# Layer 1's bias, residual and normalisation move from VectorE and GpSimd to ScalarE and GpSimd; every second unit of layer 3 has one side tap less; the final pass loads its first z tiles earlier

## The chip, the cores and the metric

The kernel runs on one core of a Trainium2 chip. Its five engines are named here as in the profile: PE (matrix products), DVE (VectorE), ACT (ScalarE), POOL (GpSimd) and SP, which only issues DMAs. Each engine executes its own instructions in order, and waits for the others by semaphores. The metric is the time of one execution on the device in microseconds (us), lower is better. A shared set of 16 DMA engines moves data between HBM and the on-chip memory (SBUF); results of PE land in PSUM.

## What is computed

The input is 16 images of 192 channels of 64 x 64 points, in float32. Four residual blocks follow one another, each with its own normalisation of the input ("norm" below: mean and inverse deviation per image and group of 6 channels):

- layer 0: x1 = x + (a small network per channel of the normalised x that ends in a likelihood);
- layer 1: x2 = x1 + W * shifts(norm(x1)) + b, where `shifts` stacks the image and its four shifts by one point, so W is five 192 x 192 products, added up;
- layer 2 (SS2D): x3 = x2 + selective scans of u = norm(x2) in four directions. Delta, B and C are projections of u; for each direction k, channel and state n = 0..15 there is a scan over the 4096 points, h = exp(delta * A) * h + (delta * u) * B, y += h * C, and u itself is added to y;
- layer 3: a depthwise convolution of norm(x3), the sum of a 3 x 3, a 5 x 5, a 1 x 7 and a 7 x 1 (29 taps together), a 192 x 192 product to z, statistics of z per channel over all 16 images, then out = x3 + min(relu(z * scale + shift), 6).

## The kernel before

**Tiling.** Two images make a pair; a pair's 2 x 192 channels lie on three tiles of 128 partitions (`NT` = 3, index j). There are eight pairs (`npair`), and L = 4096 points.

**One pair.** `pair(i)` runs `scans(i)`, the scans of layer 2, and then `layer3(i)`. The scans are 48 blocks of 1024 points x 16 states = 768 steps. One step is: the product pbt = du * pbt on DVE (pbt, B spread over the partitions, comes from PE two steps ahead, in two PSUM buffers), the scan on DVE, a copy of the last state on ACT, h * cb on POOL (cb, the C values, is loaded by SP two steps ahead), a sum over the states on PE (`ysum`), and the decay exp(delta * A) for a step three ahead on ACT. In every fourth step POOL also issues an accumulating DMA h <- h. Every 16 steps a new block begins, with a new delta and du.

**The side stream.** During the scans of pair i the front of pair i+1 runs: a Python generator that yields the work of layer 0, layer 1 (`layer1`, lines 666 to 756), the projections of layer 2, and behind these comes `ahead` of pair i (layer 3's depthwise convolution of its first tile, whose scans are done by then: matmuls with a diagonal, and a few taps `a_p` on DVE). Each step of the scans spends a credit of 1; a yield costs 1 unless it names another price: 0.52 for a matmul of layer 1, 0.57 for one of `ahead`. Work that is still left after the last step is executed behind the scans, beside nothing. Pair 0 has its front before everything else (`deep`).

**Order.** All instructions that go through an `_Engines` object with `True` are kept in program order on their engine (line 68, which is therefore the line that the profile shows for nearly all of them). The deep front, constants and the final pass are ordered by the scheduler.

**Layer 1.** The rows of x1 come in eight chunks c of 512 points (a chunk's input has ten rows, one above and one below, 640 points, 576 at the edges), double buffered as `l_xp`; `norm(c, j)` (lines 701 to 705) normalises it on POOL, one instruction by `normalise` (line 350). `on_scalar` (line 353) is the same in two ACT instructions, used elsewhere; it takes the negative mean. For each output tile jo, 10 or 15 matmuls add up in a PSUM tile `l_p`. Then `done(c, jo, p)` (707 to 715) is put on a list `after`, whose members advance by one yield after each matmul. After two yields it adds bias and residual in one DVE instruction, which reads PSUM and writes `l_xr`; a yield later it puts `bn_stats` (statistics for the next norm, DVE) on a list that is emptied at the next step, and stores x2. What is left in `after` when the matmuls are done is advanced by one for each full credit (753 to 755).

**Layer 3.** The convolution of tile 0 is made in `ahead`; tiles j = 1, 2 go in eight units u = (c, j), c = 0..3 being a quarter of the image, so even u are j = 1 and odd u j = 2. A unit's 29 taps are split: 7 (`PE_TAPS`) by diagonal matmuls into `l_p`, 9 (`GP_TAPS`) by `side`: ACT scales the window into `l_m` (the first into `l_g`), POOL adds l_g += l_m; DVE adds 12 taps in PSUM (`vector`), PE adds the side sum to PSUM (`add_side`, `l_p<-l_g`), and DVE adds the last tap and writes out (`last_tap`). The products with pw to z follow on PE, ACT copies them, DVE takes their statistics.

**Final pass** (lines 1518 to 1577). From the stored statistics (`zs`) DVE, PE and POOL compute scale and shift. Then 24 units: SP loads z (2.1 MB), ACT's queue loads x3 as `rl` (70 x 70 points with its border, 2450 KB), ACT does relu(scale, shift), DVE min and add, SP stores out. z and rl have three buffers each.

Of the kernel before, what the change touches and what calls it, by code (L numbers as in the profile page):

```python
# [11 lines left out]
F32 = mybir.dt.float32  # L12
BF16 = mybir.dt.bfloat16
AF = mybir.ActivationFunctionType
ALU = mybir.AluOpType
AX = mybir.AxisListType
PSUM = bass.MemoryType.PSUM
# [5 lines left out]
P = 128  # L23
C = 192
NT = 3
HW = 64
L = HW * HW
# [21 lines left out]
TAPS = [(3, 0), (3, 6), (0, 3), (6, 3)] + [(y, x) for y in range(1, 6) for x in range(1, 6)]  # L49
PE_TAPS = 7  # L50
GP_TAPS = 9
# [57 lines left out]
def conv_preact_kernel(ctx: ExitStack, tc: tile.TileContext, a: dict):  # L109
    nc = tc.nc  # L110
    x_in = a["x"]
    out = a["out"]
    npair = x_in.shape[0]

    def row_tiles(ap):
        return ap.rearrange("(j p) l -> p j l", p=P)
# [3 lines left out]
    S = HW + 6  # L120
    x3_d = dram.tile([npair, NT, P, S, S], F32, name="x3_d")
    y0_d = dram.tile([npair, P, L], F32, name="y0_d")
    z_d = dram.tile([npair, NT * P, L], F32, name="z_d")
    zstat_d = dram.tile([npair, P, NT * 2], F32, name="zstat_d")
# [22 lines left out]
    def load(name, shape, pool=const):  # L147
        t = pool.tile(shape, F32, name="t_" + name, tag="t_" + name)
        nc.sync.dma_start(out=t, in_=a[name])
        return t  # L150
# [9 lines left out]
    b1c = load("b1c", [P, NT])  # L160
# [47 lines left out]
    with tc.tile_pool(name="prep", bufs=1) as prep, tc.tile_pool(  # L208
        name="prep_ps", bufs=2, space=PSUM
# [115 lines left out]
    sets = [Made(n) for n in range(2)]  # L325
# [5 lines left out]
    over = ctx.enter_context(tc.tile_pool(name="over", bufs=1))  # L331

    X = over.tile([P, S, S], F32, name="X")
    Xt = over.tile([P, L], F32, name="Xt")
    zst = over.tile([P, NT, 8, 6], F32, name="zst")
    zmv = over.tile([P, NT, 2], F32, name="zmv")
    inside = slice(3, 3 + HW)
# [6 lines left out]
    def image(ap):  # L344
        return ap.rearrange("p (h w) -> p h w", w=HW)
# [4 lines left out]
    def normalise(eng, o, v, gm, rstd, j):  # L350
        eng.tensor_scalar(o, v, gm[:, j : j + 1], rstd[:, j : j + 1], ALU.subtract, ALU.mult)
# [314 lines left out]
    def layer1(o, E, ps, deep, st, gm, rstd):  # L666
        with tc.tile_pool(name="l1w", bufs=1) as w_, tc.tile_pool(name="l1x", bufs=2) as xk, tc.tile_pool(
            name="l1r", bufs=6
        ) as rk:
            w1 = w_.tile([P, len(BLOCKS), 5, P], F32, name="w1s")  # L670
            E.sp.dma_start(out=w1, in_=a["w1"])
            xps, xrs, after = {}, {}, []
# [28 lines left out]
            def norm(c, j):  # L701
                if c < 8:
                    r0, r1 = rows(c)
                    v = xps[c][:, j, r0 - 8 * c + 1 : r1 - 8 * c + 1, 1:65]
                    normalise(E.gps, v, v, gm, rstd, j)

            def done(c, jo, p):
                x = xrs.pop((c, jo))
                yield
                yield  # L710
                E.dve.scalar_tensor_tensor(x, p, b1c[:, jo : jo + 1], x, ALU.add, ALU.add)
                yield
                E.later(lambda: E.dve.bn_stats(st[:, jo, c, :], x))
                E.sp.dma_start(out=row_tiles(o.x2)[:, jo, 512 * c : 512 * c + 512], in_=x)
                yield
# [12 lines left out]
            for c in range(8):  # L728
                at = 0
                for jo in range(NT):  # L730
                    p = ps("l1_p")
                    n, last = 0, 5 * len(INTO[jo]) - 1
                    for b, ji in INTO[jo]:
                        for s, (dy, dx) in enumerate(((0, 0), (0, 1), (0, -1), (1, 0), (-1, 0))):
# [4 lines left out]
                                start=(n == 0),  # L739
                                stop=(n == last),  # L740
# [587 lines left out]
    def layer3(i, st3, o_next):  # L1328
        E = _Engines(tc, True)
        units = [(c, j) for c in range(4) for j in range(1, NT)]  # L1330
        own = PE_TAPS + GP_TAPS

        with tc.tile_pool(name="l3s", bufs=1) as stat, tc.tile_pool(name="l3y", bufs=2) as yk, tc.tile_pool(
            name="l3z", bufs=3
        ) as zk, tc.tile_pool(name="l3", bufs=2) as wk, tc.tile_pool(name="l3x", bufs=1) as xk, tc.tile_pool(
            name="l3_pt", bufs=3, space=PSUM
        ) as pt, tc.tile_pool(name="l3_pz", bufs=1, space=PSUM) as pz:
            banks = Banks(pz, 2)
            y0s, ys, gs, pss, zs, zps, stats = {}, {}, {}, {}, {}, {}, []
# [15 lines left out]
            gm = stat.tile([P, NT], F32, name="gm")  # L1355
            rstd = stat.tile([P, NT], F32, name="rstd")
            for _ in group_norm(E, st3, stat, banks, gm, rstd, aside=False):
                pass
            for rows in (slice(3, 22), slice(22, 3 + HW)):
                for j in (1, 2):  # L1360
                    v = xps[j][:, rows, inside]
# [10 lines left out]
            def side(u, taps):  # L1372
                if u < len(units):
                    c, j = units[u]
                    for n in taps:
                        tap = TAPS[PE_TAPS + n]
                        if n == 0:
                            m = gs[u] = wk.tile([P, 1024], F32, name="l3_g")
                        else:
                            m = wk.tile([P, 1024], F32, name="l3_m", bufs=3)  # L1380
                        E.act.activation(
                            image(m), window(j, 16 * c, 16, tap), AF.Copy, scale=factor(j, tap)
                        )
                        if n:
                            E.gps.tensor_tensor(gs[u], gs[u], m, ALU.add)
# [38 lines left out]

            def vector(u):
                if u < len(units):
                    for tap in TAPS[own:-1]:
                        tap_on_vector(u, tap, pss[u])

            def last_tap(u):  # L1430
# [27 lines left out]
            late, begun = [], None  # L1458
            for u in range(rounds):
# [21 lines left out]
                if u == 5 and o_next is not None:  # L1481
                    begun = begin(E, o_next, loaded, lambda: pt.tile([P, 1024], F32, name="l3_p"))
# [9 lines left out]
                end_z(E, i)  # L1492
            return begun

    def pair(i, q, more, begun, closing):

        with tc.tile_pool(name="st3", bufs=1) as p3:
            st3 = p3.tile([P, NT, 8, 6], F32, name="st3")
            nxt = None if more is None else (more, sets[1 - q])
            scans(i, sets[q], p3, st3, begun, nxt, closing)  # L1500
            return layer3(i, st3, None if more is None else sets[1 - q])

    with tc.tile_pool(name="f_ps", bufs=1, space=PSUM) as ps:
        E0 = _Engines(tc, False)
# [8 lines left out]
        begun = begin(E0, sets[0], loaded, lambda: ps.tile([P, LC], F32, name="b_v"))  # L1513
    for i in range(npair):
        begun = pair(i, i % 2, i + 1 if i + 1 < npair else None, begun, last_z(i - 1) if i else None)


    with tc.tile_pool(name="fin", bufs=1) as fin, tc.tile_pool(
        name="fin_ps", bufs=1, space=PSUM
    ) as fps:  # L1520
        same = load("same", [P, NT, NT, P], fin)
        gamma = load("gamma", [P, NT], fin)
        beta = load("beta", [P, NT], fin)
        zs = fin.tile([P, npair, NT, 2], F32, name="zs")
        nc.sync.dma_start(
            out=zs.rearrange("p i j s -> p i (j s)"), in_=zstat_d.rearrange("i p s -> p i s")
        )
        acc = fin.tile([P, NT], F32, name="acc")
        mean = fin.tile([P, NT], F32, name="zmean")
        dev = fin.tile([P, npair, NT], F32, name="dev")  # L1530
        scale = fin.tile([P, NT], F32, name="scale")
        shift = fin.tile([P, NT], F32, name="shift")
        half = fin.tile([P, NT], F32, name="mhalf")
        nc.vector.memset(half, -0.5)

        def over_images(src):
            nc.vector.tensor_reduce(acc, src.rearrange("p i j -> p j i"), AX.X, ALU.add)
            ps = fps.tile([P, NT], F32, name="over", tag="over")
            for jo in range(NT):
                for ji in range(NT):  # L1540
                    nc.tensor.matmul(
                        ps[:, jo : jo + 1],
                        same[:, ji, jo, :],
                        acc[:, ji : ji + 1],
                        start=(ji == 0),
                        stop=(ji == NT - 1),
                    )
            return ps

        ps = over_images(zs[:, :, :, 0])  # L1550
        nc.vector.tensor_scalar(mean, ps, 1.0 / (2 * npair), None, ALU.mult)
        nc.vector.tensor_tensor(
            dev, zs[:, :, :, 0], mean.unsqueeze(1).to_broadcast([P, npair, NT]), ALU.subtract
        )
        nc.vector.tensor_tensor(dev, dev, dev, ALU.mult)
        nc.vector.tensor_tensor(dev, dev, zs[:, :, :, 1], ALU.add)
        ps = over_images(dev)
        nc.vector.tensor_scalar(scale, ps, 1.0 / (2 * npair), 1e-5, ALU.mult, ALU.add)
        nc.gpsimd.tensor_tensor(scale, scale, half, ALU.pow)
        nc.vector.tensor_tensor(scale, scale, gamma, ALU.mult)  # L1560
        nc.vector.tensor_tensor(shift, mean, scale, ALU.mult)
        nc.vector.tensor_tensor(shift, beta, shift, ALU.subtract)

        with tc.tile_pool(name="last", bufs=3) as lp:
            for i in range(npair):
                for j in range(NT):
                    z = lp.tile([P, L], F32, name="zl")
                    r = lp.tile([P, S, S], F32, name="rl")
                    nc.sync.dma_start(out=z, in_=row_tiles(z_d[i])[:, j, :])
                    nc.scalar.dma_start(out=r, in_=x3_d[i, j])  # L1570
                    nc.scalar.activation(  # L1571
                        z, z, AF.Relu, bias=shift[:, j : j + 1], scale=scale[:, j : j + 1]
                    )
                    nc.vector.scalar_tensor_tensor(  # L1574
                        image(z), image(z), 6.0, r[:, inside, inside], ALU.min, ALU.add
                    )
                    nc.sync.dma_start(out=row_tiles(out[i])[:, j, :], in_=z)

def _rows(v):
# [103 lines left out]
```

## Time and profile before

| | us |
|---|---|
| median of 3 runs | 27139.78 (27134.99 to 27139.96) |
| the profiled execution | 27105.36, its span 27103.6 |
| busy PE / DVE / POOL / ACT | 23671.6 / 23419.2 / 20460.9 / 16321.5 |
| h * cb on POOL, one | 2.466 |
| scan on DVE, one | 2.28 to 2.35 |
| layer 1's bias and residual on DVE, one | 0.726, 168 in the seven fronts under scans |
| layer 1's normalisation on POOL, one | 2.67 (640 points), 2.41 (576) |
| a tap of layer 3 on DVE, one | 1.29 |

A group's line of the profile reads: line, engine, operation, output <- inputs, shapes, count | busy us, mean ns of one | idle time of the engine before it and who ended it. In a timeline a line begins with the start in us from the start of the span and the duration; `x3` says that three such instructions follow one another; brackets hold the idle time before and its releaser. "DMA share" is the mean busy share of the 16 DMA engines.

### The profile page before, as it was taken

How to read it: one execution, taken by the hardware profiler on the slowest of the kernel's cores; microseconds unless marked ns; L12 is line 12 of the kernel's file. 1: busy time of each engine (PE TensorE's matmuls, PEld its weight loads, DVE VectorE, ACT ScalarE, POOL GpSimd, SP SyncE). 2: the span in 40 equal slices, each digit the busy share in tenths (PEclk: the TensorE clock that was granted, in tenths of full speed). 3: DMA queues.
4: the chain of work that ended last, by engine and by line, in shares of the span. 5: the costliest groups of instructions: out<-in, count | busy, mean ns of one | idle time of the engine just before them, and what ended most of it. 6: DMA issues, size and time to landing. Idle time of an engine off the chain costs nothing. (4 is left out here: it accounts for less than half of the span.)

```text
span 27103.6 us, 213286 instructions
## 1 busy us (share of the span) xinstructions
PE 23671.6 (87%) x59316; PEld 9726.7 (36%) x59316; DVE 23419.2 (86%) x14897; ACT 16321.5 (60%) x23587; POOL 20460.9 (75%) x10424
## 2 busy tenths in 40 slices
PE   8899988999889998999889998899988999866773
PEld 3333333333333333333333333333333333322231
DVE  1289998899889998899989999889988999899994
ACT  7478455774568644785557845577456864544443
POOL 2388877888778877788778887778877887777773
PEclk9899999999999999999999999999999999988996
DMA  4479875798768975789757987579876897567766
GB/s 108 122 213 232 222 221 158 219 219 221 209 173 223 221 223 163 210 225 224 224 152 216 227 222 221 160 218 220 221 208 173 222 221 223 160 192 193 200 194 277
DMA packets 2050521, 5524.18 MB, mean 204 GB/s; under 512 B 556024, under 2 KB 556248, under 8 KB 2032816
## 3 DMA queue, kind: packets, MB, share of 16 engines
q1 hardware_dynamic: 1824688, 4644.91, 58.2%
q0 software_dynamic: 221184, 805.40, 15.9%
q10 hardware_dynamic: 3456, 60.21, 0.5%
q8 instruction: 474, 7.77, 0.1%
q14 instruction: 719, 5.89, 0.1%
HBM read 3943.05 MB, written 358.46 MB: 159 GB/s over the span
## 5 line engine op out<-in xcount | busy, mean ns | idle before, releaser
L68 POOL TENSOR_TENSOR h<-h,cb 128x1024 f32<-128x1024 f32 x6144 | 14852.9, 2466 | 4210.7 <-ACT state L68 3490.1
L68 DVE TENSOR_TENSOR_SCAN h<-dA,state,pbt 128x1024 f32<-128x1024 f32 x4608 | 10806.3, 2345 | 759.9 <-DMA h<-h 163.0
L68 PE MATMUL ysum<-h,ident 128*128 128x512 f32 x18432 | 9091.7, 617 | 110.3 <-DMA h<-h 58.4
L68 DVE TENSOR_TENSOR pbt<-du,pbt 128x1024 f32<-128x1024 f32 x6144 | 7434.0, 1210 | 591.6 <-PE pbt L68 439.5
L68 ACT ACTIVATE dA<-delta,t_alog 128x1024 f32<-128x1024 f32 x6144 | 7034.8, 1146 | 16.9 <-DMA z_d<-z 7.6
L68 PEld LDWEIGHTS ysum<-h,ident 128*128 128x128 f32 x18432 | 3630.7, 198 | 4332.6 <-issue 3892.2
L68 ACT COPY state<-h 128x1 f32<-128x1 f32 x6144 | 1141.8, 186 | 6216.4 <-DVE h L68 6201.4
L68 PE MATMUL pbt<-bp,pick 96*128 96x512 bf16 x8192 | 2558.1, 395 | 1507.8 <-DVE h L68 1483.7
L68 DVE TENSOR_TENSOR_SCAN h<-dA,pbt 128x1024 f32<-128x1024 f32 x1536 | 3509.0, 2284 | 259.4 <-DMA h<-h 72.8
L68 PE MATMUL p<-m,wms 128*96 128x512 f32 (+1 forms) x5376 | 2661.4, 596 | 40.8 <-ACT t L68 23.1
L68 PEld LDWEIGHTS <-pick 96*128 96x128 bf16 x8192 | 692.8, 100 | 4335.5 <-DVE h L68 2746.1
L68 PE MATMUL l_p<-l_xp,w1s 128*128 128x512 f32 x3920 | 1855.0, 593 | 0.0
L68 POOL DMA_DIRECT2D h<-h x1536 | 1356.9, 883 | 496.8 <-POOL h L68 431.0
L68 PE MATMUL pbt<-bp,pick_mix 96*128 96x512 bf16 x4096 | 1266.3, 391 | 494.8 <-DVE h L68 492.0
L68 PE MATMUL p<-m,wts 96*128 96x512 f32 x2688 | 1373.5, 623 | 217.0 <-ACT m L68 215.3
L68 ACT ACT_TABLE_LOAD x1089 | 1397.2, 1283 | 19.2
L68 PE MATMUL p<-t,wts 96*128 96x512 f32 x2688 | 1374.4, 592 | 0.0
L68 POOL TENSOR_TENSOR l_g<-l_g,l_m 128x1024 f32<-128x1024 f32 x512 | 1229.5, 2405 | 112.1 <-ACT l_m L68 78.6
L68 ACT ACTIVATE m<-p,bias 96x512 f32<-96x512 f32 x1344 | 907.2, 675 | 654.6 <-PE p L68 654.1
L68 PE MATMUL a_p<-a_x,diag 128*128 128x512 f32 x2688 | 1276.4, 599 | 1.6 <-ACT a_x L68 1.6
L68 PEld LDWEIGHTS p<-m,wms 128*96 128x96 f32 (+1 forms) x5376 | 944.8, 177 | 796.2 <-issue 352.9
L68 ACT ACTIVATE m<-m,bias,sp 96x512 f32<-96x512 f32 x1344 | 1078.4, 803 | 204.7 <-DMA m<-l_xn 186.9
(278 smaller groups left out, 21228.6 us busy)
## 6 DMA issues: line engine op xcount, KB each, us to landing
cb<-cp_d SPq DMA_DIRECT2D x2048, 512.0 KB
cb<-c_d SPq DMA_DIRECT2D x2048, 512.0 KB
h<-h POOLq DMA_DIRECT2D x1536, 512.0 KB, 6.9
cb<-cp_d SPq DMA_DIRECT2D x2048, 256.0 KB
cb<-c_d SPq DMA_DIRECT2D x2048, 256.0 KB
m<-l_xn SPq DMA_DIRECT2D x3072, 128.0 KB
bp<-bp_d SPq DMA_DIRECT2D x384, 192.0 KB
rl<-x_d ACTq DMA_DIRECT2D x24, 2450.0 KB
```

What stands on the lines that cost most here:

```text
L68: return self._tc.keep_in_program_order(call(*args, **kw))
```

## The change

Four edits. In layer 1 under scans the input is normalised by two ACT instructions; the PSUM tile is read by ACT, with the bias, into a new tile `l1_t`, POOL adds that to the residual a yield later, and the statistics and the store come two yields after that (before: one yield after the sum). In the deep front DVE normalises instead of POOL. In layer 3 odd units have eight side taps, and DVE takes the ninth. The final pass stands in the last pair's `pair`: the z loads of the units 0 to 2 are issued before its layer 3, z has four buffers (two of its own, two in the places of `xn` and `Xt`), rl four, and only the 64 rows of x3 inside the border are loaded.

```diff
@@ layer1
+            less = w_.tile([P, NT], F32, name="less1")
+            E.act.activation(less, gm, AF.Copy, scale=-1.0)
...
-                    normalise(E.gps, v, v, gm, rstd, j)
+                    if deep:
+                        normalise(E.dve, v, v, gm, rstd, j)
+                    else:
+                        on_scalar(E, v, v, less, rstd, j)
 
             def done(c, jo, p):
                 x = xrs.pop((c, jo))
                 yield
                 yield
-                E.dve.scalar_tensor_tensor(x, p, b1c[:, jo : jo + 1], x, ALU.add, ALU.add)
-                yield
+                if deep:
+                    E.dve.scalar_tensor_tensor(x, p, b1c[:, jo : jo + 1], x, ALU.add, ALU.add)
+                    yield
+                else:
+                    t = xk.tile([P, 512], F32, name="l1_t", tag="l1_t")
+                    E.act.activation(t, p, AF.Identity, bias=b1c[:, jo : jo + 1])
+                    yield
+                    E.gps.tensor_tensor(x, x, t, ALU.add)
+                    yield
+                    yield
                 E.later(lambda: E.dve.bn_stats(st[:, jo, c, :], x))
                 E.sp.dma_start(out=row_tiles(o.x2)[:, jo, 512 * c : 512 * c + 512], in_=x)
                 yield
@@ layer3
-        own = PE_TAPS + GP_TAPS
+        on_side = lambda u: GP_TAPS - u % 2
...
                         tap = TAPS[PE_TAPS + n]
+                        if n >= on_side(u):
+                            continue
...
-                    for tap in TAPS[own:-1]:
+                    for tap in TAPS[PE_TAPS + on_side(u) : -1]:
@@ pair
-            return layer3(i, st3, None if more is None else sets[1 - q])
+            if more is not None:
+                return layer3(i, st3, sets[1 - q])
+            with tc.tile_pool(name="zl", bufs=2) as pool:
+                got = [load_z(u, pool) for u in range(3)]
+                layer3(i, st3, None)
+                final(got, pool)
+
+    def load_z(u, pool):
+
+        i, j = divmod(u, NT)
+        if u % 4 < 2:
+            z = pool.tile([P, L], F32, name="zl", tag="zl")
+        else:
+            z = over.tile([P, L], F32, name="zl", tag=("xn", "Xt")[u % 4 - 2])
+        nc.sync.dma_start(out=z, in_=row_tiles(z_d[i])[:, j, :])
+        return z
@@ final pass
-        with tc.tile_pool(name="last", bufs=3) as lp:
-            for i in range(npair):
-                for j in range(NT):
-                    z = lp.tile([P, L], F32, name="zl")
-                    r = lp.tile([P, S, S], F32, name="rl")
-                    nc.sync.dma_start(out=z, in_=row_tiles(z_d[i])[:, j, :])
-                    nc.scalar.dma_start(out=r, in_=x3_d[i, j])
+            with tc.tile_pool(name="last", bufs=4) as lp:
+                for u in range(NT * npair):
+                    i, j = divmod(u, NT)
+                    z = got[u] if u < len(got) else load_z(u, pool)
+                    r = lp.tile([P, HW, S], F32, name="rl")
+                    nc.scalar.dma_start(out=r, in_=x3_d[i, j][:, inside, :])
```

More of the change, by code (lines that the diff above doesn't have):

```diff
@@ L1493, in layer3, with pair @@
             return begun
-    def pair(i, q, more, begun, closing):
+    def pair(i, q, more, begun, closing, last=None):
         with tc.tile_pool(name="st3", bufs=1) as p3:
@@ new lines, in final, with over_images @@
+    def final(got, pool):
+        with tc.tile_pool(name="fin", bufs=1) as fin, tc.tile_pool(
+            name="fin_ps", bufs=1, space=PSUM
+        ) as fps:
+            same = load("same", [P, NT, NT, P], fin)
+            gamma = load("gamma", [P, NT], fin)
+            beta = load("beta", [P, NT], fin)
+            zs = fin.tile([P, npair, NT, 2], F32, name="zs")
+            nc.sync.dma_start(
+                out=zs.rearrange("p i j s -> p i (j s)"), in_=zstat_d.rearrange("i p s -> p i s")
+            )
+            acc = fin.tile([P, NT], F32, name="acc")
+            mean = fin.tile([P, NT], F32, name="zmean")
+            dev = fin.tile([P, npair, NT], F32, name="dev")
+            scale = fin.tile([P, NT], F32, name="scale")
+            shift = fin.tile([P, NT], F32, name="shift")
+            half = fin.tile([P, NT], F32, name="mhalf")
+            nc.vector.memset(half, -0.5)
+            def over_images(src):
+                nc.vector.tensor_reduce(acc, src.rearrange("p i j -> p j i"), AX.X, ALU.add)
+                ps = fps.tile([P, NT], F32, name="over", tag="over")
+                for jo in range(NT):
+                    for ji in range(NT):
+                        nc.tensor.matmul(
+                            ps[:, jo : jo + 1],
+                            same[:, ji, jo, :],
+                            acc[:, ji : ji + 1],
+                            start=(ji == 0),
+                            stop=(ji == NT - 1),
+                        )
+                return ps
+            ps = over_images(zs[:, :, :, 0])
+            nc.vector.tensor_scalar(mean, ps, 1.0 / (2 * npair), None, ALU.mult)
+            nc.vector.tensor_tensor(
+                dev, zs[:, :, :, 0], mean.unsqueeze(1).to_broadcast([P, npair, NT]), ALU.subtract
+            )
+            nc.vector.tensor_tensor(dev, dev, dev, ALU.mult)
+            nc.vector.tensor_tensor(dev, dev, zs[:, :, :, 1], ALU.add)
+            ps = over_images(dev)
+            nc.vector.tensor_scalar(scale, ps, 1.0 / (2 * npair), 1e-5, ALU.mult, ALU.add)
+            nc.gpsimd.tensor_tensor(scale, scale, half, ALU.pow)
+            nc.vector.tensor_tensor(scale, scale, gamma, ALU.mult)
+            nc.vector.tensor_tensor(shift, mean, scale, ALU.mult)
+            nc.vector.tensor_tensor(shift, beta, shift, ALU.subtract)
+            with tc.tile_pool(name="last", bufs=4) as lp:
[4 more added lines that the diff above has]
+                    nc.scalar.dma_start(out=r, in_=x3_d[i, j][:, inside, :])
+                    nc.scalar.activation(
+                        z, z, AF.Relu, bias=shift[:, j : j + 1], scale=scale[:, j : j + 1]
+                    )
+                    nc.vector.scalar_tensor_tensor(
+                        image(z), image(z), 6.0, r[:, :, inside], ALU.min, ALU.add
+                    )
+                    nc.sync.dma_start(out=row_tiles(out[i])[:, j, :], in_=z)
@@ L1515, in conv_preact_kernel @@
         begun = pair(i, i % 2, i + 1 if i + 1 < npair else None, begun, last_z(i - 1) if i else None)
[L1518 to L1562, printed above, removed]
-        with tc.tile_pool(name="last", bufs=3) as lp:
-            for i in range(npair):
-                for j in range(NT):
-                    z = lp.tile([P, L], F32, name="zl")
-                    r = lp.tile([P, S, S], F32, name="rl")
-                    nc.sync.dma_start(out=z, in_=row_tiles(z_d[i])[:, j, :])
-                    nc.scalar.dma_start(out=r, in_=x3_d[i, j])
[L1571 to L1577, printed above, removed]
```

## The prediction

> **What bounds the kernel now.** I read the engine totals first, then the stages that the change touches, each by its own table of busy time, and last the instructions around each edit.
>
> ```profile
> span 27103.6 us, 213286 instructions
> PE 23671.6 (87%) x59316; PEld 9726.7 (36%) x59316; DVE 23419.2 (86%) x14897; ACT 16321.5 (60%) x23587; POOL 20460.9 (75%) x10424
> ```
>
> PE and DVE are level over the whole span, so the totals decide nothing. By stretches (PE, PEld, DVE, ACT, POOL busy; clock; DMA share; GB/s), first a layer 1 under its scan steps, then a piece of the final pass:
>
> ```profile
> 6097.00:6701.00 604.00, 555.26 (x1427) 231.58 (x1427) 580.29 (x373) 252.41 (x366) 495.24 (x252) 0.99 0.85 222
> 26850.00:26900.00 50.00, 0.00 (x0) 0.00 (x0) 13.71 (x5) 11.95 (x4) 0.00 (x0) 0.50 1.01 418
> ```
>
> Layer 1 is DVE's: 96% busy in 159 scan steps of 3.80 us. PE has 555 of 604, so some room, ACT plenty. The final pass is the DMA engines' alone. What DVE does there, in order:
>
> ```profile
> 6411.17 2.29 DVE L68 TENSOR_TENSOR_SCAN h<-dA,pbt 128x1024 f32<-128x1024 f32 x1
> 6413.38 0.73 DVE L68 SCALAR_TENSOR_TENSOR l_xr<-l_p,t_b1c,l_xr 128x512 f32<-128x512 f32 x1
> 6414.02 1.22 DVE L68 TENSOR_TENSOR pbt<-du,pbt 128x1024 f32<-128x1024 f32 x1
> 6415.37 2.29 DVE L68 TENSOR_TENSOR_SCAN h<-dA,pbt 128x1024 f32<-128x1024 f32 x1
> 6417.57 1.21 DVE L68 TENSOR_TENSOR pbt<-du,pbt 128x1024 f32<-128x1024 f32 x1
> 6418.69 0.68 DVE L68 BATCH_NORM_STATS2 fst<-l_xr 128x6 f32<-128x512 f32 x1
> ```
>
> Product and scan back to back; an instruction of layer 1 in between lengthens its step by itself.
>
> **Layer 1, DVE's part: -109.** From scan start to scan start a plain step takes 3.58 us, one with the bias-and-residual instruction 4.23: 0.65 each (0.73 by itself, less the overlap with its neighbours). 168 of them go: -109.2. PE must then follow at 604 - 24 x 0.65 = 588 us a stage with 555 busy, 94%; its work goes by the step, 3.49 against 3.70, so it still fits.
>
> **Layer 1, ACT and POOL.** ACT gains per stage 24 x (2 x 0.83 + 0.68) = 56 us (0.83 for 640 elements, between 0.71 for 512 and 1.15 for 1024; 0.68 from its other PSUM evictions) on 252 of 588. It computes decays three steps ahead, which covers that, and the 5.2 us that POOL waited once for the stage's first load, now ACT's wait. POOL loses the normalisation and gains the add:
>
> ```profile
> L68 POOL TENSOR_SCALAR l_xp<-l_xp,fgm,frstd 128x640 f32<-128x640 f32 x126 | 336.7, 2672 | 0.0
> L68 POOL TENSOR_TENSOR l_x<-l_x,sg 128x512 f32<-128x512 f32 x168 | 213.0, 1268 | 14.0
> ```
>
> so it comes out 24 x 1.3 = 31 us a stage lighter. Nothing of this ends on the path, if DVE does not wait for it.
>
> **Layer 1, the new wait: +28.** The statistics of an output (0.69, on DVE) now read what POOL added. DVE is in order: while they wait, the next scan waits, and behind it state copy, h*cb and everything else. The add is queued behind POOL's h*cb of its step:
>
> ```profile
> 6414.03 2.65 POOL L68 TENSOR_TENSOR h<-h,cb 128x1024 f32<-128x1024 f32 x1
> ```
>
> This one starts 0.6 us after its scan's end because an accumulate DMA is issued ahead of it; in the other three of four steps it is 0.2 to 0.4. With 2.4 for h*cb and 1.3 for the add, the add ends 4.0 after its scan's end, in a fourth step 4.9, and where a new u product is made on POOL (2.4) about 6.4. The statistics are due two steps on, by the rows above about 4.6 after that scan's end. Aligning the 24 outputs of a stage with the steps gives a floor of 2.1 us a stage (15 in all: only the fourth and the u steps wait), and a ceiling of 8 (56) if also the stage's first output meets the late cb load (POOL waited 6.7 us there) and two more are a step unlucky. I take 4 a stage, +28, nearer to the floor, because the stall on PE that DVE has there today (6.4 us, longest 3.2) can absorb part. The gain side: at 0 the sum is 28 lower.
>
> **Layer 1, the longer way out: +21.** An output needs two advances more after its last matmul, so the stage is two steps longer and the last two steps' work of the next front (`ahead`) falls behind the scans, uncovered. There PE sets the pace:
>
> ```profile
> 4199.88 2.34 DVE L68 SCALAR_TENSOR_TENSOR a_p<-a_x,wc,a_p 128x512 f32<-128x512 f32 x3 [8.93 <-PE a_p L68]
> 4218.98 2.34 DVE L68 SCALAR_TENSOR_TENSOR a_p<-a_x,wc,a_p 128x512 f32<-128x512 f32 x3 [16.75 <-PE a_p L68]
> ```
>
> 19.1 us for 22 matmuls, and a step's credit buys 1/0.57 of them: 1.52 us. 2 x 1.52 x 7 pairs = +21.3 (0 if rounding of the credits takes the steps in, 21 more if group statistics come late too).
>
> **Layer 3: +21.5.** Every odd unit gives one tap from ACT and POOL to DVE. A tap costs 1.32 start to start (12 in 15.86).
>
> ```profile
> 4271.97 15.86 DVE L68 SCALAR_TENSOR_TENSOR l_p<-X,wc,l_p 128x1024 f32<-128x1024 f32 x12
> 4290.62 1.28 DVE L68 SCALAR_TENSOR_TENSOR l_y<-X,wc,l_p 128x1024 f32<-128x1024 f32 x1 [2.80 <-PE l_p L68]
> ```
>
> ```profile
> 4287.97 2.62 PE L68 MATMUL l_p<-l_g,ident 64*64 64x512 f32 x8 [4.22 <-DVE l_p L68]
> 4330.56 1.94 PE L68 MATMUL l_p<-l_g,ident 64*64 64x512 f32 x8
> 4411.70 3.68 PE L68 MATMUL l_p<-l_g,ident 64*64 64x512 f32 x8 [11.04 <-DVE l_p L68]
> ```
>
> PE's add of the side sum starts 0.15 after DVE's last tap in units 1 and 7 (DVE ends 4287.82 and 4411.55): no slack, 1.32 each. In 3 and 5 PE comes 1.96 and 2.45 later, at its own pace (no idle before 4330.56): hidden. 2 x 1.32 x 8 pairs = 21.1, and 0.3 in the last pair, where unit 5 has 1.2. What POOL is relieved of buys nothing: its side sum of unit 1 ends 4279.05, of unit 7 4403.00, over 8 us ahead. The chain does name "POOL l_g" (under 0.5%); that is a tie of 0.04 us in the last pair.
>
> **Final pass: -16.** It moves 24 x (2.10 + 2.51 + 2.10) = 160.9 MB. The r loads get 64 of 70 rows (-5.2 MB), three z loads (6.3) go under layer 3, where the DMA engines are 11% busy. What is lost again is the start:
>
> ```profile
> 26715.68 0.39 SPq L1525 DMA_DIRECT2D zs<-zstat_d  x1
> ```
>
> ```profile
> 26735.75 0.19 DVE L1537 TENSOR_REDUCE acc<-zs 128x3 f32<-128x24 f32 x1 [21.74 <-DMA zs<-zstat_d]
> ```
>
> The tiny zs load takes 20 us, in which the z and r loads issued beside it move 7.1 MB; all of DVE's and ACT's work waits for it, the first write comes at 26755. From there 147.1 MB at 428 GB/s give 26755 + 344 + 5 = 27104, the span. Afterwards 149.4 MB in all: with z3 and four r's (11.3 MB) beside zs, which then lands at 26743, the end is 14 earlier; with two r's 25. Between them -19, and +3 for z loads that come ahead of layer 3's own on SP's queue: xp1, diag and pw (0 to 10; DVE's first use waits 0.99 for pw today). By bounds: -30 to +5.
>
> The Trainium skill bears on this (*DMA: Bandwidth & Descriptors*, section *Queues, rings and completion order*): each DMA engine goes round its queue rows a packet at a time, so a small load is slowed by every large one in another row. That speaks for four r's holding zs up; by it alone the final part would be worth -11 and the sum 5 less than below.
>
> **Deep front: -2.** Its first normalisation goes from POOL (2.3) to DVE (about 0.5) with PE waiting; after that PE is 245 of 248 us busy.
>
> **Sum.** -109 + 28 + 21 + 21.5 - 16 - 2 = -56.5. The profiled run took 27105.4 (span 27103.6), 34 below the median of the runs; taken off the median: 27083.
>
> **Rivals.** *A, POOL stays as late as now (slower).* Its h*cb end 3.8 us after the scan on average in this stage, not 2.7; if the add's wait there follows this, the wait is near 0.7 an output, 115 in all in place of 28: 27170. For: POOL is 82% busy and waits for state copies and cb loads in bursts. Against: it sheds 31 us a stage. It becomes slower than now from 28 + 57 = 85, 0.5 us an output, and slower by 0.2% from 0.83.
> *B, the final pass gains nothing:* zs is held up by all that is queued and layer 3 starts 5 later: 27083 + 21 = 27104.
> *C, the side taps on POOL bind layer 3,* as the chain's entry could mean: 32 taps of 2.44 = -78 in place of +21.5: 26983. The 8 us of slack speak against it.
> *D, the small terms fall well:* waits at the floor, final pass -27, tail steps rounded off for half: 27083 - 13 - 11 - 10 = 27049.
>
> **How the numbers follow.** A measurement of this kernel tells about 0.2%, 54 us, from no change: 27086 and 27194 are the limits, and the forecast lies on the first. Chances: forecast 0.52, its own range 27060 to 27115 (halves either side of 27086); A 0.22, of which a third beyond 0.83 us an output; B 0.09; C 0.04; D 0.13. Faster: 0.26 + 0.04 + 0.13 + 0.01 = 0.44; slower 0.08; same 0.48. The range leaves out C and the far part of A: 27040 to 27175.
>
> **What would show it.** In the new trace's layer 1 stages: steps of at most 3.98 us with one statistics instruction; DVE's statistics waiting on POOL's l_xr, 0.1 to 0.3 us a time; ACT near 308 us. After the scans: two or more matmuls of `ahead` more per pair. In layer 3: 13 taps in 17.2 us in odd units, the adds of units 1 and 7 1.32 later, those of 3 and 5 not. In the final pass: zs landing later, the first write at 26751 to 26762 on today's scale. It would be wrong if the statistics wait over half a microsecond each, or if DVE, freed, waits for PE instead.

## The result, and the profile after

The changed kernel takes 27193.17 us (median of 15 runs, 27170.78 to 27210.26) against 27139.71 for the kernel before, measured beside it (27114.17 to 27151.42): ratio 1.0019, 95% interval 1.0011 to 1.0027. It is 53 us slower; forecast were 57 us less, 27083, and a range that ended at 27175.

The profiled executions are 27105.4 before and 27174.6 after, 34 and 19 below their medians, so the two traces differ by 69 where the medians differ by 53. The page of the changed kernel:

```profile
span 27172.8 us, 213249 instructions
PE 23742.7 (87%) x59316; PEld 9747.1 (36%) x59316; DVE 23368.1 (86%) x14785; ACT 16642.2 (61%) x24067; POOL 20125.6 (74%) x10368
```

The work moved as counted: DVE is 51 us less busy (168 bias instructions go, 109 without the parts in which they overlapped their neighbours; 32 taps of layer 3 with 42 and the deep normalisation with 15 come), ACT 321 more, POOL 335 less. The same stretch of layer 1 as was shown of before, 604 us (PE, PEld, DVE, ACT, POOL busy; clock; DMA share; GB/s):

```profile
6114.00:6718.00 604.00, 556.92 (x1428) 233.57 (x1427) 566.10 (x350) 303.28 (x441) 467.60 (x249) 0.99 0.85 220
```

DVE is 14 us less busy, yet the stretch is no shorter: DVE waits instead. The groups of the edit over the whole trace, with the idle time before them and its releaser in the last column:

```profile
L68 POOL TENSOR_TENSOR l_xr<-l_xr,l_t 128x512 f32<-128x512 f32 x168 | 232.9, 1386 | 50.3 <-ACT state L68 50.3
L68 DVE BATCH_NORM_STATS2 fst<-l_xr 128x6 f32<-128x512 f32 x168 | 115.5, 688 | 150.1 <-POOL l_xr L68 150.1
```

150.1 us of DVE's time before the statistics of layer 1, all of it for POOL's sum. In the kernel before, these 168 instructions waited 0.0:

```profile
L68 DVE BATCH_NORM_STATS2 fst<-l_xr 128x6 f32<-128x512 f32 x168 | 115.0, 685 | 0.0
```

To see where the time went I aligned the two traces by scan steps, which are the same 768 in each of the eight pairs. Layer 1 lies in steps 430 to 600 of the first seven. Differences to the trace of before, in us:

| trace of | before the first scan | steps 0-430 | 430-600 | 600-767 | between the pairs | last pair's scans | behind the last scan | sum |
|---|---|---|---|---|---|---|---|---|
| the changed kernel | +3.6 | -6.8 | 0.0 | +23.6 | +55.3 | +6.0 | -12.5 | +69.2 |
| only layer 3 changed | +4.3 | -0.6 | +12.3 | +8.5 | +23.5 | +1.6 | +6.2 | +55.7 |
| only the final pass changed | +4.8 | +6.5 | +17.7 | +5.7 | +3.3 | +3.1 | -14.9 | +26.3 |
| statistics of ACT's tile | +4.0 | +13.4 | -99.3 | +23.3 | +52.3 | +3.5 | -12.2 | -15.1 |
| statistics four advances later | +1.6 | +5.8 | -121.5 | -3.8 | +95.6 | +3.2 | -13.5 | -32.6 |
| the changed kernel, way out cheaper | +0.9 | -8.8 | +13.6 | +7.4 | -6.5 | +1.0 | -13.2 | -5.5 |
| the fastest but one (below) | -0.3 | -3.2 | -113.1 | +36.0 | +1.6 | +2.3 | -15.7 | -92.5 |

The two rows without an edit in layer 1 show how far a column of single traces can be trusted: the trace of before was a quick one, and up to 18 us in 430-600 are scatter (there it is DVE's waits that are longer, by 11.0 and 17.6). So layer 1 gained nothing where 81 were forecast, and the work between the pairs (what is left of the front, and layer 3) cost 55.

### The profile page after: what moved, and what is told of

Its sections match the earlier page's. It is cut to its first block, busy times and chain, and to the rows that moved or that the text cites. A ratio compares the mean times of both kernels' runs of the same rounds, so it can differ in the third digit from the quotient of the medians.

```text
span 27172.8 us, 213249 instructions
## 1 busy us (share of the span) xinstructions
PE 23742.7 (87%) x59316; PEld 9747.1 (36%) x59316; DVE 23368.1 (86%) x14785; ACT 16642.2 (61%) x24067; POOL 20125.6 (74%) x10368
## 5 line engine op out<-in xcount | busy, mean ns | idle before, releaser
L68 ACT ACTIVATE dA<-delta,t_alog 128x1024 f32<-128x1024 f32 x6144 | 7035.2, 1146 | 17.7 <-DMA z_d<-z 7.4
L68 POOL TENSOR_TENSOR l_g<-l_g,l_m 128x1024 f32<-128x1024 f32 x480 | 1154.4, 2409 | 168.2 <-ACT l_m L68 83.7
```

Of the source, the lines that this page charges most:

```text
L68: return self._tc.keep_in_program_order(call(*args, **kw))
```

## The experiments

**Which part loses.** Three kernels take the change apart; a fourth keeps all of it, but takes away what the statistics wait for. Layer 1's edit alone (the deep front's included):

> Layer 1's edit alone (layer 3 and the final pass as before). From the trace of the changed kernel: +17 in the scans under which layer 1 runs (-109 for the DVE instruction, waits of the statistics +150, some 24 of PE stalls gone) and +25 behind the scans, so +42, 27182. If the tap of layer 3 or the final pass were the loss and layer 1 gained as forecast, 27080 to 27090.

Layer 3 alone (`on_side` as in the diff):

> Only the eighth side tap of odd units goes to DVE. Forecast of the prediction +21.5 (27161); by the trace of the changed kernel, where layer 3 is 3.8 a pair longer, +30 (27170). If POOL's side taps bound layer 3, some -78 (27062).

The final pass alone, with the earlier z loads:

> Only the final pass is changed, with the z loads ahead of the last layer 3. The prediction has -16 (27124), the trace of the changed kernel -16 as well behind the last tap. If the earlier z loads hold layer 3 up, near 0.

The changed kernel with

```diff
-                E.later(lambda: E.dve.bn_stats(st[:, jo, c, :], x))
+                E.later(lambda: E.dve.bn_stats(st[:, jo, c, :], x if deep else t))
```

> The changed kernel with the statistics of layer 1 taken of ACT's tile l1_t and not of POOL's sum: DVE waits for ACT alone, everything else stays. The statistics are then not those of x2. If the wait of DVE on POOL's add is the loss, most of its 150 goes, all but some 20 where ACT itself is late: -130, 27063. If the loss is PE or ACT (DVE's room was never usable), the waits come back under another name and the time stays near 27190.

| | median, us | against before | 95% interval of the ratio |
|---|---|---|---|
| layer 1 alone | 27192.7 | +52.9 | 1.0011 to 1.0029 |
| layer 3 alone | 27161.9 | +22.1 | 1.0000 to 1.0018 |
| final pass alone | 27124.8 | -15.0 | 0.9985 to 1.0002 |
| statistics of ACT's tile | 27078.0 | -61.8 | 0.9968 to 0.9987 |

The runs of this document come from five rounds, each with the kernel before beside it; its medians there were 27134.5 to 27146.4, so a difference between two changed kernels of different rounds is uncertain by up to 12 us more.

The three parts add up to +60, the change to +53. Layer 3 and the final pass came out at their forecasts (+21.5, -16) to within 1 us of the medians; the intervals are some 24 us wide to either side, so that much closeness is in part luck. By the medians all of the error is in layer 1. The fourth kernel shows what it is: with the same instructions on every engine, but DVE not waiting for POOL, the time falls by 115 us.

How the saved instruction and the new wait balance can be followed on DVE alone. Its waits in steps 430 to 600 of the seven pairs sum to 87.5 us before and 198.3 in the changed kernel: +110.8, against 168 x 0.65 = 109.2 saved; the stretch should change by +1.6, and it changed by 0.0. The 150 of the statistics are not all new: waits for PE's pbt fell from 38.1 to 18.6 there and those for decays from 32.2 to 20.8, because a DVE that stands still lets PE and ACT get ahead. In the kernel with the statistics of ACT's tile the sum is 104.7 (17 more than before), so -92; measured -99.3.

**Where POOL is late, and why.** The waits are not spread over the 24 outputs of a stage. In the second front 15 outputs wait nothing, five 0.5 to 1.5 us, and four 6.3, 3.2, 4.9 and 2.4 us, at steps 444, 452, 503 and 555. The same four come back in the other fronts but the first, whose outputs lie at other steps; they are 104 of the 126 us in the fronts 2 to 7. The third of them, first on DVE, then on POOL:

```profile
6380.31 0.69 DVE L68 BATCH_NORM_STATS2 st<-X 128x6 f32<-128x512 f32 x1
6385.89 0.69 DVE L68 BATCH_NORM_STATS2 fst<-l_xr 128x6 f32<-128x512 f32 x1 [4.89 <-POOL l_xr L68]
```

```profile
6367.59 2.35 POOL L68 TENSOR_TENSOR h<-h,cb 128x1024 f32<-128x1024 f32 x1 [0.54 <-DMA cb<-c_d]
6375.50 2.37 POOL L68 TENSOR_TENSOR h<-h,cb 128x1024 f32<-128x1024 f32 x1 [5.56 <-ACT dA L68]
6378.69 2.37 POOL L68 TENSOR_TENSOR h<-h,cb 128x1024 f32<-128x1024 f32 x1 [0.82 <-DMA cb<-c_d]
6381.36 0.89 POOL L68 DMA_DIRECT2D h<-h  x1 [0.30 <-POOL h L68]
6381.98 2.65 POOL L68 TENSOR_TENSOR h<-h,cb 128x1024 f32<-128x1024 f32 x1
6384.28 1.57 POOL L68 TENSOR_TENSOR l_xr<-l_xr,l_t 128x512 f32<-128x512 f32 x1
```

The h * cb of 6375.50 is that of step 500, whose scan had ended at 6368.17 and whose state copy 0.26 later. The profile names ACT's dA as its releaser, which it has no use for: it also waits for its cb, and that was late on SP:

```profile
6357.87 3.32 SPq L68 DMA_DIRECT2D cb<-c_d  x4
6361.29 0.53 SPq L68 DMA_DIRECT2D x_d<-l_xr  x1
6361.92 7.50 SPq L68 DMA_DIRECT2D l_xr<-x_d  x3
6369.48 1.09 SPq L68 DMA_DIRECT2D cb<-c_d  x2
```

```profile
SPq L68 <- DMA x_d<-l_xr: 5.7, 1, 5.7
```

The second line of the timeline is the store of x2 of an earlier output, the third the load of the next chunk's residual. Its last part goes into the tile that is being stored, and by SP's waits of these 8 us it waits 5.7 for that store; the cb loads of step 500 stand behind it. After that three h * cb and a DMA issue are queued ahead of the add, which ends at 6385.85, while DVE was ready at 6381.0. The other three places: at 444 SP issues the three loads of the next chunk's input for 6.5 us, a cb load behind them is late (POOL waits 6.45 us) and a u product precedes the add; at 452 the edit's PSUM read stands on ACT behind a copy of X that waits 3.57 us for PE's sums, and POOL waits for ACT (in the kernel with the statistics of ACT's tile DVE still waits 1.85 us there, for ACT); at 555 a u product precedes the add. These three are read from the trace; no run tests them one by one.

The reading of step 503 was tried: the residuals loaded five matmuls later, nothing else.

```diff
-                            if at == 8:
+                            if at == 13:
                                 load_r(c + 1)
```

> The changed kernel, but the next chunk's residual is loaded after matmul 13 of a chunk, not 8, so that SP need not wait for the store of the tile that it loads into. In the trace of the changed kernel that wait is 16.2 us in the second front (longest 5.7, ahead of the late cb loads of step 500). If it is what makes POOL late there, the wait of the statistics at step 503 (5.6 a front) mostly goes and the 150 fall to some 115: 27160. If ACT's work at these steps does it, the waits and the time stay (27193).

27157.5 (ratio 0.9996 to 1.0014), 36 less than the changed kernel; against the kernel before beside it, +11 where the changed kernel has +53. The two intervals overlap, so the place where the wait shrank says more than the time. The 150 fell to 108, or 114 with one wait for which the profile names a cb load; at step 503 DVE waits 1.4 to 2.5 us where it waited 4.9 to 6.9, while 444 has 2.5 to 6.4 and 452 and 555 are as they were. So part of the wait is a loop that the edit closes itself: its later store holds SP, SP holds cb, cb holds POOL, and POOL the next sum. In the kernel before SP waited for such stores too, but 7.2 us in the second front and not 16.2, 2.5 at most and not 5.7.

Was this lateness new? The end of h * cb behind the end of its scan, in the fronts 2, 4 and 7:

| step | before | changed kernel |
|---|---|---|
| median of steps 430-600 | 3.2, 3.5, 3.3 | 2.7, 2.7, 2.8 |
| 444 | 10.3, 8.3, 8.0 | 9.6, 9.3, 10.3 |
| 452 | 3.9, 3.9, 3.9 | 6.6, 6.7, 6.7 |
| 503 | 7.4, 6.8, 6.9 | 8.9, 9.8, 10.0 |
| 555 | 3.5, 3.5, 3.5 | 5.8, 5.8, 5.8 |

At 452 and 555 the changed kernel's number contains the add itself, which stands ahead of that h * cb. At 444 of front 2 the 10.3 of before are these two lines, the scan's end (6146.07) and the end of h * cb (6156.38):

```profile
6143.74 2.33 DVE L68 TENSOR_TENSOR_SCAN h<-dA,state,pbt 128x1024 f32<-128x1024 f32 x1
6154.03 2.35 POOL L68 TENSOR_TENSOR h<-h,cb 128x1024 f32<-128x1024 f32 x1
```

Typically POOL is more punctual than before, as forecast. But at the two worst places it was 7 to 10 us late in the kernel before as well, where no instruction of DVE waited for it.

**Does the wait shrink if the statistics come later?** The changed kernel with four more advances between add and statistics (two scan steps), and one with two more (one step):

```diff
                     E.gps.tensor_tensor(x, x, t, ALU.add)
                     yield
                     yield
+                    yield
+                    yield
+                    yield
+                    yield
...
-                            if at == 8:
+                            if at == 9 + 4:
                                 load_r(c + 1)
```

> The changed kernel with the statistics and the store of x2 four advances (two steps) later behind POOL's add, and the next residual load five advances later so that SP doesn't wait for that store. If DVE's wait on the add is the loss, at most 10 of its 150 are left, while layer 1's way out is four steps longer, 4 x 1.52 x 7 = +43: some -70 against the changed kernel, 27125. If the wait moves on with the statistics (POOL late without limit), 27193 + 43 = 27236.

(With two: two yields more and `at == 11`.)

> As the run with the statistics four advances later, but only two (one step, 3.6 us) later than in the changed kernel. If a wait is simply what POOL's add is late by, the waits of 6 shrink to some 2.5 and those of 3.3 and 2.4 vanish: 25 to 30 of the 150 left; two steps more behind the scans, +21: between the changed kernel (27193) and that run (27073) less its own tail, some 27090.

Measured: 27073.0 with four (ratio 0.9967 to 0.9986), 27076.3 with two (0.9969 to 0.9987): both beat the kernel before, by 62 and 60 us, and the changed one by 120 and 117 (115 and 113 against the kernel before beside each). The waits of DVE for POOL's sum are gone with four, and 8.6 us with two (17.4 more where the trace names a cb load as the releaser). DVE's longest waits over all fronts (releaser: us in all, times, longest), first of the kernel with four, where the statistics no longer appear:

```profile
DVE pbt L68 <- PE pbt L68: 446.8, 562, 5.4
DVE a_p L68 <- PE a_p L68: 256.4, 20, 16.8
DVE h L68 <- DMA h<-h: 187.1, 101, 6.9
DVE h L68 <- ACT dA L68: 161.6, 452, 2.7
```

against the changed kernel's:

```profile
DVE pbt L68 <- PE pbt L68: 415.3, 507, 6.2
DVE a_p L68 <- PE a_p L68: 214.5, 14, 16.8
DVE h L68 <- DMA h<-h: 194.7, 83, 6.3
DVE h L68 <- ACT dA L68: 163.9, 453, 3.2
DVE fst L68 <- POOL l_xr L68: 150.1, 66, 6.9
```

The second line is the price, the front's leftover behind the scans (below). Both kernels came out better than expected, by 52 and 14 us. In steps 430-600 they save 121.5 and 121.0, where 109 for the instruction and 5 and 1 from the waits make 114 and 110. Of the rest, the kernel with four is 27 shorter than the changed one in steps 600-767, but that with two is 14 longer there; why is not known. Both of them also load the residuals later. That alone, with the statistics where they were, was worth 36 and left 114 us of the wait; how the 117 to 120 divide between the load and the distance from add to statistics, no run separates.

**Whose lateness is it, ACT's or POOL's own?** Each half of layer 1's edit alone: the normalisation on ACT, the rest as before; and the eviction by ACT and add by POOL, with the normalisation left on POOL.

> Only the normalisation of layer 1's input goes to ACT (the deep one to DVE); bias and residual stay one DVE instruction. POOL gets 63 us a stage lighter, ACT 40 heavier, DVE does the same work: 27140, no change. If ACT's two more instructions hold up state copies and decays by themselves, slower by 20 and more.

> Only bias by ACT and add by POOL; the normalisation stays on POOL, which is then 31 us a stage heavier than before and 63 heavier than with layer 1's whole edit (27193). If POOL's own queue makes the add late, the statistics wait longer than 150, 200 or more: 27230 to 27260. If it is ACT's normalisation that makes POOL late (state copies behind it), they wait less, some 100: 27150.

Normalisation alone: 27123.4, 0.9986 to 1.0004, no change that can be told. It costs nothing on ACT and gains nothing on DVE. Eviction and add alone: 27222.3 (1.0020 to 1.0043), 88 over before and 30 over layer 1's whole edit (35 against the kernel before beside each). Its statistics in DVE's waits over all fronts:

```profile
DVE fst L68 <- POOL l_xr L68: 173.6, 69, 8.8
```

The wait grows with POOL's load, but by 25 only, not by 50 and more: with layer 1's whole edit it is 149.0, and with the waits that the profile puts down to a cb load the two sums are 184.5 and 161.9. The rival that ACT's normalisation makes POOL late falls (the wait would have shrunk); POOL's own load is a part of it, but the bulk of the wait comes from the places above, which are there with either engine. In the kernel with the normalisation alone, which has neither the later store nor the add, h * cb of steps 443 and 502, behind which the adds of the two worst places stand, still ends 9.9, 8.3, 9.8 and 7.6, 5.8, 6.9 us behind its scan (fronts 2, 4 and 7).

**The longer way out.** The changed kernel with cheaper advances at the end of layer 1:

```diff
             while after:
-                yield
+                yield 0.52
                 advance()
```

> The changed kernel with the last seven advances of layer 1 at 0.52 credit, not 1: its front is 3.4 steps shorter. By the price of the prediction (1.52 us of the work behind the scans a step) -3.4 x 1.52 x 7 = -36: 27157. If those steps are hidden anyway, 27193.

27117.8 (ratio to before 0.9985 to 1.0003), 75 less than the changed kernel (72 against the kernel before beside each); the work between the pairs shrinks by 62, not 36. The end of `ahead` behind the last scan, mean of the seven pairs: 42.9 us before, 46.5 in the changed kernel, 39.2 here, 49.3 and 53.5 with the statistics two and four advances later. So two steps more are 3.6 us a pair (3.04 forecast), but it goes in lumps: here 75 of the trace's matmuls are left and 92 in the changed kernel. The trace shows each matmul of the program as two, so these are 8.5, where 3.4 steps of credit buy 6. Why so many is open. The waits of the statistics stay (138.8).

**A version that beats both.** The changed kernel without layer 3's edit, with the statistics four advances later and the cheaper way out:

> The changed kernel without the edit of layer 3, statistics and store four advances later as in the run with later statistics, and the last advances of layer 1 at 0.52 credit each, not 1: 11 x 0.52 = 5.7 steps of way out against 5 before. -109 + 20 in layer 1, +7 behind the scans, -16 final pass: 27140 - 98 = 27042; some 15 more if the projections behind layer 1 stay slower as in the traces of the changed kernel: 27057.

27015.0 (27010.8 to 27029.7), ratio 0.9957, 0.9944 to 0.9969: 119 below the kernel before beside it, and 27 less than expected. The end of `ahead` is back at 42.9. On top of it layer 3 was turned round: units 1 and 7 get a tenth side tap, DVE eleven taps.

```diff
-        on_side = lambda u: GP_TAPS - u % 2
+        on_side = lambda u: GP_TAPS + (u in (1, 7))
...
-                side(u, range(7, GP_TAPS))
+                side(u, range(7, GP_TAPS + 1))
```

> The fastest version so far with layer 3 turned round: units 1 and 7 get a tenth side tap and DVE eleven taps. If DVE sets the end of those units and POOL has 8 us to spare, as the prediction read, -2 x 1.32 x 8 = -21: 26994. If POOL binds as the chain's entry says, slower, up to +39 (2.44 a unit).

27003.2 (26999.4 to 27014.2), ratio 0.9952, 0.9939 to 0.9964. From DVE's first to last tap layer 3 is 162.4 us a pair against 165.4, -24 in eight pairs by the trace, -12 by the medians, which scatter as much. That POOL binds is refuted, since a tap more on POOL did not lengthen layer 3 here, and a tap less (layer 3 alone) did not shorten it; the size stays between the two.

## Why the prediction was wrong

- **DVE's removed instruction, -109:** held. The change of steps 430-600 is that of DVE's work and waits, to 2 us in the changed kernel and to 7 in those with the statistics of ACT's tile and with four advances.
- **The new wait, +28 between 15 and 56:** this is the step that failed. Measured 150, or 111 net of the waits it replaced. "The add ends 4.0 after its scan's end" took the punctual step for all but those with an accumulate DMA or a u product, and one late cb. The form of the sum was right (add's end against the statistics' turn 4.6 later), the lateness put into it was not: with the lag that the trace of before shows at steps 444 and 503, 8.0 to 10.3 and 6.8 to 7.4, the same sum gives 4.7 to 7.0 and 3.5 to 4.1; measured 6.0 to 6.9 and 4.9 to 6.1 in the same fronts. Rival A used the mean lag and came to 115 for all outputs; that was near in size, but in part by luck: the waits come from a few outputs and not from all, and over the 159 steps of the stretch the mean lag is 4.4 us, not 3.8. The point given for "slower", 0.5 us an output, was crossed: 0.89.
- **"Can absorb part":** it did, 31 us (pbt and decays), as an amount far from enough.
- **Way out, +21:** held: 3.6 us a pair, 25, for four matmuls of the program where the prediction had 3.5.
- **Layer 3, +21.5:** held, in the mechanism too. The runs say +22.1 (0 to 49), the trace of that kernel +2.7 a pair from first to last tap (164.9 to 167.6). DVE's taps of unit 1 and PE's adds of units 1, 3, 5 and 7 in the changed kernel:

```profile
4286.27 17.18 DVE L68 SCALAR_TENSOR_TENSOR l_p<-X,wc,l_p 128x1024 f32<-128x1024 f32 x13
```

```profile
4303.60 3.68 PE L68 MATMUL l_p<-l_g,ident 64*64 64x512 f32 x8 [5.37 <-DVE l_p L68]
4346.55 1.93 PE L68 MATMUL l_p<-l_g,ident 64*64 64x512 f32 x8 [0.20 <-DVE l_p L68]
4388.28 1.93 PE L68 MATMUL l_p<-l_g,ident 64*64 64x512 f32 x8
4429.02 3.68 PE L68 MATMUL l_p<-l_g,ident 64*64 64x512 f32 x8 [12.37 <-DVE l_p L68]
```

  Unit 5 hides its tap as read (no idle before 4388.28); unit 3 has become a tie, 0.20 us of waiting.

- **Final pass, -16:** the size held (-15.0 alone, -41 to +5), one reason did not. zs did not land later:

```profile
26808.91 0.37 SPq L1541 DMA_DIRECT2D zs<-zstat_d  x1
26817.48 0.20 DVE L1553 TENSOR_REDUCE acc<-zs 128x3 f32<-128x24 f32 x1 [17.51 <-DMA zs<-zstat_d]
```

  It is issued 228 us behind the last scan, 216 before, and lands 9 us later instead of 20, since z3 was issued 11 us ahead of it and only the first r load runs beside it; the second r load follows 20 us after the first, and the DMA engines idle for half of that. The first use of zs comes 236 us behind the last scan in both kernels, the first store 256. So, by this reading, what is gained is the smaller volume, less what this idle time gives back:

```profile
26809.00:26829.00 20.00, 7.94 (x36) 7.83 (x36) 1.74 (x10) 0.31 (x1) 0.86 (x1) 0.50 0.33 117
```

  (DMA share 0.33 in these 20 us.) In the packets one sees how a small load is held up. zs is 24 KB in 1024 packets of 24 bytes, on SP's queue (q1); the r load on ACT's queue (q10) has packets of 18 KB. From 26811 to 26815 the two go one for one, and from 26816 to 26817, when r ends, the rest of zs passes at once (packets, MB, share of 16 engines):

```profile
q10 hardware_dynamic: 92, 1.65, 97.4%
q1 hardware_dynamic: 92, 0.00, 1.3%
```

```profile
q1 hardware_dynamic: 879, 0.02, 49.4%
q10 hardware_dynamic: 13, 0.04, 9.0%
```

  In the kernel before it is 86 to 86 packets from 26729 to 26733, and zs outlasts two r loads. The Trainium skill (*DMA: Bandwidth & Descriptors*, section *Queues, rings and completion order*) has the engines go round the queue rows by packets, and these counts agree with it. The reason that the prediction drew from it was sound; but four r loads beside zs, for which it was used, never came about.
- **Deep front, -2:** not seen. PE's wait for the first normalised input is 6.2 us against 6.3, and the first scan is 3.6 later, 2.7 of which were there before layer 1 began, in work that the change leaves alone.

What stays open: steps 600-767, behind layer 1, are 23 to 50 us longer in the traces of seven of the ten kernels with ACT's eviction, 7 to 10 in two and 4 shorter in one. They hold no edit (only with the statistics two and four advances later do the last of these reach steps 600 and 602); the front's position against the scan steps is shifted there, and which of its loads or sums then meet badly was not settled.

## What to carry to other kernels

When an instruction on the engine that sets the pace is split so that its last part waits for another engine, look up how late that engine is at the very steps where the parts land, not on average: here the median was 3 us, four places of 6 to 10 decided it, and the two worst stood in the trace of before. The cure tried here is distance, not speed: the same split with the reader one scan step later, and the load that must follow it moved along, turned +53 into -60. What the distance costs at the end of a pipelined stage has its own price, and it can be bought back there.

## What was not expected

A wait on one engine partly pays for others: with DVE standing still for 150 us at the statistics, its waits for PE and for decays in the same steps fell from 70.3 to 39.4. And the single profiled execution misleads at this size: kernels without any edit in layer 1 showed +12 and +18 us in its steps against the trace of before, so that terms of 20 us cannot be told from single traces; even the medians of 5 to 31 runs have intervals of 22 to 34 us to either side.
